# Splitting the second sum of a LayerNorm folding into pieces and spreading them over layer 0 of a two-way GRU

## The chip, the cores and the metric

The kernel runs on one core of a Trainium2 chip. The core has five engines with an instruction stream each: TensorE (PE in the profile; its weight loads are PEld), VectorE (DVE), ScalarE (ACT), GpSimd (POOL) and SyncE (SP), which issues nearly all DMAs. They run side by side and wait for one another through semaphores. The metric is the time of one execution on the device in microseconds (us), as the median of several runs; lower is better.

## What is computed

The input `x` has 8 sequences (b) of 512 tokens with 512 features. The block adds a fused two-way recurrent stack to it, and then a feed-forward part with ternary weights:

```python
def _mingru(x, Wz, bz, Wh, bh):
    z = sigmoid(x @ Wz.T + bz)
    h_tilde = tanh(x @ Wh.T + bh)
    a = clip(1.0 - z, 1e-8, 1.0 - 1e-8)
    return _linear_scan(a, z * h_tilde)        # h[t] = a[t] h[t-1] + z[t] h_tilde[t]

def _stack(x, ...):                            # 4 layers
    h = x
    for i in range(4):
        h_new = _mingru(h, Wz[i], bz[i], Wh[i], bh[i])
        if i > 0:
            h_new = h_new + h
        h = _layernorm(h_new, gamma, beta)
    return h

# block:
h_fwd = _stack(layernorm(x));  h_bwd = flip(_stack(flip(layernorm(x))))
x = x + concat(h_fwd, h_bwd) @ fusion_W.T + fusion_b
x = x + ffn(layernorm(x))                      # 512 -> 2048 -> gelu -> layernorm -> 512
```

All four weight and bias arguments of a layer are the same two arrays here, so one product serves the sigmoid and the tanh, and the two directions share it in layer 0.

## The kernel before

**Tiles and stages.** Features lie on the 128 partitions, in four chunks of 128; a tile is 128 features by 512 tokens in f32. Four stages follow one another: loads and the normalisation of `x` (to about 15 us), four recurrent layers for two sequences at a time with both directions, the fusion product, and the feed-forward part.

**One item of a layer** is a sequence, a direction and a layer: `layer(s, l)` with `s = (b, d)` (L541). It has four chunks, and each is one slot: four matmuls into an accumulator `u` in PSUM (L459), three activations on ScalarE that read it (`factors`, L473), and on VectorE a clamp, a product, a scan and an addition (L481 to L487, L552). Layer 0 has its own code (`first_layer`, L491), since both directions share the product: eight chunks for the first two sequences, `f0` and `f1`, each scaled by VectorE (L515) before the activations and scanned twice. The scaling of a chunk of `f1` comes two slots after its matmuls (`lag` 2), so its accumulator stays in use for that long.

**Normalisation.** The scanned tiles are transposed to token rows (`turned`, L307, into `pt`, two buffers), VectorE takes their statistics (L169), GpSimd the power (L176), ScalarE writes a normalised token tile (L187), which frees the `pt` buffer; then four token tiles are transposed back (`back`, L318, into `pf`, two buffers) and ScalarE writes them with `gamma` and `beta` applied (L329).

**The order of the work** is written out by hand (L114). `slot` (L437) emits a chunk's matmuls, then what `stages` holds as due (`factors`, `scans`, `resid`), then shares of the two queues `turns` and `backs`; `now` counts slots. `ready` (L251) lets no new token tile begin while ten are held (`held`, `TOK` = 10). The engines take their instructions in this order. Slots 0 to 7 are `f0 + f1` (L728); slots 8 to 11 are item (0, 0) of layer 1, 12 to 15 item (0, 1), and 16 begins item (1, 0).

**PSUM.** The pool `ps_u` (L229) has four buffers of one bank each. The accumulators of the layers, those of layer 0 and those of the folding all come from it.

**The folding.** The last layer's LayerNorm is not applied to the tokens. Instead its `gamma` goes into the fusion weights `fw`, its mean out of them, and its `beta` into the fusion bias. `both` (L119) is a table with `beta` and `gamma` of each feature repeated over 64 columns each, written by two VectorE copies after slot 7 (L730). `fold_sums(d)` (L667) multiplies it with the half of `fw` that belongs to direction d: four matmuls into `pfold`, then a ScalarE copy into a tile of the token pool. It is called after item (0, 0) and after item (0, 1) of layer 1 (L763). The products `pm` and `pb` (L682, L692) read both results in layer 2, from 145 us on.

**The first loads** on SP's queue are the weights and inputs of sequence 0, the GRU bias `gb`, four row tiles of sequence 1 (L148), its transposed input `xT` (L149), `gamma` and `beta` (L150), then the fusion bias and weights, the other layers' weights and the feed-forward's norm. Two VectorE statistics in the first slots read the first two of those row tiles. The program takes eight DMA completion semaphores in turn, so a load is issued once the load eight before it has landed.

Of the kernel before, what the change touches and what calls it, by code (L numbers as in the profile page):

```python
# [9 lines left out]
F32 = mybir.dt.float32  # L10
# [6 lines left out]
P = 128  # L17
# [7 lines left out]
def kernel(  # L25
# [26 lines left out]
    nc = tc.nc  # L52
    B, S, H = x.shape
    L = gru_wT.shape[0]
    F = fc_wT.shape[1]
    NC_ = H // P
# [13 lines left out]
    tokp = ctx.enter_context(tc.tile_pool(name="tok", bufs=TOK))  # L70
# [23 lines left out]
    def load_x(use, b, t):  # L94
        xs[use, b, t] = xsp.tile([P, H], F32, tag="xs", name=f"x{use}_{b}_{t}")
        nc.sync.dma_start(out=xs[use, b, t], in_=x[b, ts(t, P), :])
# [6 lines left out]
    def load_xT(b):  # L103
        xT[b] = hp.tile([P, NC_, S], F32, tag="h", name=f"xT_{b}")
        nc.sync.dma_start(out=xT[b], in_=xt[b].rearrange("(c p) s -> p c s", p=P))

    gb = const.tile([P, L, NC_], F32, name="gb")
    gam = const.tile([P, NC_], F32, name="gam")
    bet = const.tile([P, NC_], F32, name="bet")
# [9 lines left out]
    both = fusp.tile([P, NC_, 2, 64], F32, name="both")  # L119
    picks = []  # L120
    for i in range(2):
        s = fusp.tile([P, P], F32, name=f"fpick{i}")
# [17 lines left out]
    for first, second in (  # L140
# [3 lines left out]
        for q, (load, at) in ((nc.scalar, first), (nc.sync, second)):  # L144
            load(q, at)
    nc.sync.dma_start(out=gb, in_=gru_b)
    for t in range(NT):
        load_x("n", 1, t)  # L148
    load_xT(1)  # L149
    nc.sync.dma_start(out=gam, in_=gamma)  # L150
    nc.sync.dma_start(out=bet, in_=beta)
    fw = fusp.tile([P, 2 * NC_, H], F32, name="fw")
    nc.sync.dma_start(out=fb, in_=fus_b.broadcast_to([P, H]))
    nc.sync.dma_start(out=fw, in_=fus_wT.rearrange("(c p) h -> p c h", p=P))
# [72 lines left out]
    with rec:  # L227
        gp = rec.enter_context(tc.tile_pool(name="gate", bufs=3))
        ps_u = rec.enter_context(tc.tile_pool(name="ps_u", bufs=4, space=PSUM))  # L229
# [10 lines left out]
        held = [0]  # L240
# [232 lines left out]
        def factors(u, z, l, o, name):  # L473
            t = gp.tile([P, S], F32, tag="t", bufs=2, name=f"t_{name}")
            a = gp.tile([P, S], F32, tag="a", name=f"a_{name}")
            nc.scalar.activation(a, u, AF.Sigmoid, bias=ngb[:, l, o : o + 1], scale=-1.0)  # L476
            nc.scalar.activation(t, u, AF.Tanh, bias=gb[:, l, o : o + 1])  # L477
            nc.scalar.activation(z, u, AF.Sigmoid, bias=gb[:, l, o : o + 1])  # L478
            return a, t
# [11 lines left out]
        def first_layer(b, lag=0):  # L491


            zf, zb = [], []

            def chunk(o):
                def work():
                    while zlive[0] + 2 > ZT:
                        slot(None, 2)
                    zlive[0] += 2  # L500
                    name = f"{b}_0_{o}"
                    u = ps_u.tile([P, S], F32, tag="u", name=f"u_{name}")
                    for c in range(NC_):
                        nc.tensor.matmul(  # L504
                            u, lhsT=gw[0][:, c, ts(o, P)], rhs=xT[b][:, c, :],
                            start=(c == 0), stop=(c == NC_ - 1),
                        )
                        if (b, o, c) in midway:
                            midway.pop((b, o, c))()

                    wait = 1 if (b, o) == (0, 0) else 0

                    def scaled():
                        z = zp.tile([P, S], F32, tag="z", name=f"z_{name}")
                        nc.vector.tensor_tensor(z, u, scale[b], ALU.mult)  # L515
                        a, t = factors(z, z, 0, o, name)

                        def scans():
                            product(a, z, t)
                            f = zp.tile([P, S], F32, tag="z", name=f"zf_{name}")  # L520
                            scan(f, a, z, False)
                            zf.append(f)
                            if o == NC_ - 1:
                                state[b, 0] = xT.pop(b)
                                norm((b, 0), zf, f"{b}0_0", 2 if b == 1 else 1, 2 if b < 2 else 1)

                            def backward():
                                scan(z, a, z, True)
                                zb.append(z)
                                if o == NC_ - 1:  # L530
                                    norm((b, 1), zb, f"{b}1_0", 2 if b == 1 else 1, 2 if b < 2 else 1)
                            if b == 0:
                                stages.append((now[0] + 1, "resid", backward))
                            else:
                                backward()
                        stages.append((now[0] + 1 - wait, "scans", scans))
                    stages.append((now[0] + lag + wait, "factors", scaled))
                return work
            return [chunk(o) for o in range(NC_)]
# [124 lines left out]

        folded = {}

        def fold_sums(d):  # L667

            ps = ps_u.tile([P, H], F32, tag="u", name=f"pfold_{d}")
            for c in range(NC_):  # L670
                nc.tensor.matmul(
                    ps, lhsT=both[:, c, :, :].rearrange("p i r -> p (i r)"), rhs=fw[:, d * NC_ + c, :],
                    start=(c == 0), stop=(c == NC_ - 1),
                )
            folded[d] = tokp.tile([P, H], F32, tag="tok", name=f"fold_{d}")
            held[0] += 1
            nc.scalar.copy(folded[d], ps)

        def fold(d):

# [39 lines left out]
        end = take(xturns)  # L720
# [4 lines left out]
        take(xturns)  # L725
        midway[0, 1, 0] = lambda: take(xbacks)()
        f0, f1 = first_layer(0), first_layer(1, 2)
        for i, work in enumerate(f0 + f1):  # L728
            slot(work, 4 if i == NC_ + 1 else 2, i > NC_ + 1)
        for i, v in enumerate((bet, gam)):  # L730
            nc.vector.tensor_copy(both[:, :, i, :], v.unsqueeze(2).broadcast_to([P, NC_, 64]))
        for b in range(0, B, 2):
            last_pair = b + 2 == B
            if b == 0:
                for name, part in (("fc", fc_part), ("pw", proj_part)):
                    for i in range(NW):
                        absolute(part, i, name)
                    tots = []
                    extra.append([None, lambda n=name, tots=tots: tots.append(total(n))])
                    extra.append([None, lambda n=name, tots=tots: threshold(n, tots[0])])  # L740
                for name, part in (("fc", fc_part), ("pw", proj_part)):
                    for i in range(NW):
                        quantised(part, i, name)
            for l in range(1, L):
                if last_pair:
                    load_fc(l - 1)
                    if l == 1:
                        combined()
                        load_pw(0)
                for s in ((b, 0), (b, 1), (b + 1, 0), (b + 1, 1)):  # L750
                    if l == L - 1 and not last_pair and s[1] == 0:
                        norm_x(s[0] + 2, now[0])
                    if l == L - 1 and s[1] == 0:
                        load_pair("f", s[0])
                    if l == L - 2 and not last_pair and s[1] == 1:
                        load_pair("n", s[0] + 2)
                        load_xT(s[0] + 2)
                    if last_pair and s == (b, 1) and l == L - 2:
                        load_y(0)
                    if last_pair and s == (b, 0) and l == L - 1:  # L760
                        norm_y(0)
                    layer(s, l)
                    if b == 0 and l == 1 and s[0] == 0:  # L763
                        fold_sums(s[1])
                    if b == 0 and l == 2:
                        if s[0] == 0:
                            fold(s[1])
                        elif s[1] == 0:
                            fold_bias()
            if last_pair:  # L770
                load_fc(L - 1)


            firsts = [] if last_pair else first_layer(b + 2) + first_layer(b + 3)
            for i in range(2):
                for t, tile_ in enumerate(fusion(b + i)):
                    slot(tile_, 2, True)
                    for _ in range(2 if i == 0 and t % 2 == 0 else 1):
                        if firsts:
                            slot(firsts.pop(0))  # L780
                if last_pair and i == 0:
                    load_pw(1)
                    load_pw(2)
# [20 lines left out]
    for i in range(2):  # L804
        plain = tokp.tile([P, H], F32, tag="tok", name=f"plain{i}")[:, 0:P]
        nc.vector.memset(plain, 0.0)
        for j in range(2):
            r = 64 * i + 32 * j
            nc.vector.memset(plain[r : r + 1, :], 1.0)
        s = const.tile([P, P], F32R, name=f"pick{i}")  # L810
# [137 lines left out]
    for j in range(ends):  # L948
        b, k = divmod(j, NF)
# [81 lines left out]
```

## Time and profile before

| | |
|---|---|
| median of three runs | 1717.03 us (1716.73 to 1717.18) |
| the profiled execution: time, span of the core | 1717.09 us, 1715.1 us |
| PE busy | 1703.4 us, 99% of the span |
| DVE, ACT busy | 1452.0 us (85%), 1073.7 us (63%) |
| first sum of the folding: first matmul, ACT copy | 62.7 us, 66.4 us |
| second sum of the folding: first matmul, ACT copy | 87.4 us, 91.6 us |
| the two copies that write `both` | 47.3 us and 47.5 us, 0.28 us each |
| issue and landing of `gamma`, of `beta` | 11.7 to 17.3 us, 12.1 to 17.5 us |

The profile is of one execution. Its times are counted from the start of the span; the rest of an execution lies around the span. A line of the timeline or of the chain of work gives the start, the length, the engine, the line in the kernel, the operation and the tiles (written, then read), and in brackets how long the engine had been idle before and for whom it had waited. Buffer numbers are left out of tile names. A matmul of 128x512 in f32 shows as two instructions. Matmuls overlap, so their ends are modelled, and the busy share of PE says less than its waits.

### The profile page before, as it was taken

Reading aid. Unit: us, or ns where it says so; the run is one execution under the profiler, and the core shown is the slowest. Engines: PE = TensorE matmul, PEld = TensorE weight load, DVE = VectorE, ACT = ScalarE, POOL = GpSimd, SP = SyncE. Lnnn points to the kernel's source line nnn. Section 1 sums busy time; section 2 is a strip of 40 time slices with the busy share of each in tenths; the row PEclk is TensorE's granted clock in tenths of the full one; section 3 lists DMA queues with packets and bytes.
Section 4 is the critical chain, followed back from the end, with each engine's and each line's share of the span. In section 5 each row is a group of like instructions: output and inputs, shape, how many; then the busy total and the mean of one; then the engine's idle time right before and its main releaser. Section 6 shows DMA issues by size and latency. Waiting matters only on the chain.

```text
span 1715.1 us, 19769 instructions
## 1 busy us (share of the span) xinstructions
PE 1703.4 (99%) x6440; PEld 1042.3 (61%) x6440; DVE 1452.0 (85%) x2863; ACT 1073.7 (63%) x1856; POOL 214.0 (12%) x334
## 2 busy tenths in 40 slices
PE   9999999999999999999999999999999999999999
PEld 4455554555555445555545555554688888888887
DVE  7989989889998998999899899996568768768877
ACT  5898873468886246888624688860366566566654
POOL 2111111111111111111111111110000000000000
PEclk9999999999999999999999999999999999999999
DMA  7002221160000115000011201202201101100100
GB/s 270 19 25 81 99 86 43 56 202 1 1 13 19 56 56 202 1 1 18 14 55 68 105 9 41 74 1 96 76 1 49 50 0 50 49 16 35 50 19 32
DMA packets 46599, 91.75 MB, mean 53 GB/s; under 512 B 5280, under 2 KB 5536, under 8 KB 45472
## 3 DMA queue, kind: packets, MB, share of 16 engines
q1 hardware_dynamic: 45488, 88.78, 15.1%
q10 hardware_dynamic: 1008, 1.70, 0.3%
q8 instruction: 51, 0.84, 0.2%
q14 instruction: 52, 0.43, 0.1%
HBM read 65.30 MB, written 25.17 MB: 53 GB/s over the span
## 4 chain that ended last, share of the span: by engine, by line
PE 87%; DVE 10%; ACT 1%; issue 1%; DMA 1%; POOL 0%; DVEq 0%; ACTq 0%
PE u L459 32%; PE po L870 14%; PE ph L843 14%; PE pu L586 12%; PE pt L314 6%; PE u L504 5%; PE pf L323 4%; DVE z L487 3%; DVE st L169 1%; DVE z L483 1%; PE py L212 1%; DVE zf L487 1%; DVE z L552 1%; DVE a L482 1%; DVE mv L171 0%
## 5 line engine op out<-in xcount | busy, mean ns | idle before, releaser
L459 PE MATMUL u<-h,gw 128*128 128x512 f32 x768 | 345.5, 592 | 0.0
L459 PE MATMUL u<-xT,gw 128*128 128x512 f32 x768 | 345.4, 593 | 0.0
L487 DVE TENSOR_TENSOR_SCAN z<-a,z 128x512 f32<-128x512 f32 x224 | 274.1, 1224 | 7.6
L459 PEld LDWEIGHTS u<-h,gw 128*128 128x128 f32 x768 | 138.7, 190 | 139.2 <-issue 138.9
L459 PEld LDWEIGHTS u<-xT,gw 128*128 128x128 f32 x768 | 138.7, 190 | 139.2 <-issue 138.2
L476 ACT ACTIVATE a<-u,ngb 128x512 f32<-128x512 f32 x192 | 131.6, 685 | 142.4 <-PE u L459 141.8
L169 DVE BATCH_NORM_STATS2 st<-pt 128x6 f32<-128x512 f32 x256 | 177.2, 692 | 40.8 <-PE pt L314 40.3
L176 POOL TENSOR_TENSOR rs<-ve,mhalf 128x1 f32<-128x1 f32 x192 | 122.7, 639 | 703.7 <-DVE nmu L180 665.4
L870 PE MATMUL po<-pwq,ghi 128*128 128x512 f32 x512 | 202.7, 396 | 0.0
L843 PE MATMUL ph<-yhi,fcq 128*128 128x512 f32 x512 | 199.7, 390 | 0.0
L870 PE MATMUL po<-pwq,glo 128*128 128x512 f32 x512 | 199.6, 390 | 0.0
L843 PE MATMUL ph<-ylo,fcq 128*128 128x512 f32 x512 | 199.4, 389 | 0.0
L847 ACT ACTIVATE g<-ph 128x512 f32<-128x512 f32 x128 | 76.4, 597 | 186.4 <-PE ph L843 186.4
L483 DVE TENSOR_TENSOR z<-z,t 128x512 f32<-128x512 f32 x224 | 153.4, 685 | 9.4 <-ACT z L478 9.4
L187 ACT ACTIVATE tok<-pt,nmr,rs 128x512 f32<-128x512 f32 x192 | 149.2, 777 | 6.4
L858 DVE TENSOR_TENSOR acc<-acc,g 128x512 f32<-128x512 f32 x112 | 77.3, 690 | 84.7 <-ACT g L847 83.8
L478 ACT ACTIVATE z<-u,gb 128x512 f32<-128x512 f32 x192 | 132.2, 689 | 0.0
L477 ACT ACTIVATE t<-u,gb 128x512 f32<-128x512 f32 x192 | 130.7, 681 | 0.0
L314 PEld LDWEIGHTS pt<-ident,z 128*128 128x128 f32 x640 | 78.6, 141 | 80.2 <-issue 47.5
L504 PE MATMUL u<-xT,gw 128*128 128x512 f32 x256 | 115.0, 593 | 1.0 <-DVE gw L716 0.8
L586 PE MATMUL pu<-fw,xT 128*128 128x512 f32 x256 | 115.2, 593 | 0.0
L586 PE MATMUL pu<-fw,h 128*128 128x512 f32 x256 | 115.1, 592 | 0.0
(150 smaller groups left out, 2559.8 us busy)
## 6 DMA issues: line engine op xcount, KB each, us to landing
xf<-in_x_dram SPq DMA_DIRECT2D x32, 256.0 KB, 5.8
x<-xf SPq DMA_DIRECT2D x32, 256.0 KB, 2.0
xy<-x SPq DMA_DIRECT2D x32, 256.0 KB, 4.1
xn<-in_x_dram SPq DMA_DIRECT2D x31, 256.0 KB, 4.5
out_dram<-xy SPq DMA_DIRECT2D x31, 256.0 KB, 2.0
xT<-in_xt_dram SPq DMA_DIRECT2D x7, 1024.0 KB, 7.5
fca<-in_fc_wT_dram SPq DMA_DIRECT2D x16, 256.0 KB, 3.0
pwa<-in_proj_wT_dram SPq DMA_DIRECT2D x16, 256.0 KB, 2.7
```

The lines of the kernel that those rows point to most:

```text
L169: nc.vector.bn_stats(st, src)
L187: nc.scalar.activation(dst, src, AF.Identity, bias=nmr, scale=rs)
L314: nc.tensor.transpose(pt[:, ts(c, P)], zs[c][:, ts(t, P)], ident)
L459: nc.tensor.matmul(u, lhsT=gw[l][:, c, ts(o, P)], rhs=h[:, c, :], start=(c == 0), stop=(c == NC_ - 1),)
L476: nc.scalar.activation(a, u, AF.Sigmoid, bias=ngb[:, l, o : o + 1], scale=-1.0)
L478: nc.scalar.activation(z, u, AF.Sigmoid, bias=gb[:, l, o : o + 1])
L483: nc.vector.tensor_tensor(z, z, t, ALU.mult)
L487: nc.vector.tensor_tensor_scan(dst[:, d], a[:, d], z[:, d], 0.0, ALU.mult, ALU.add)
L504: nc.tensor.matmul(u, lhsT=gw[0][:, c, ts(o, P)], rhs=xT[b][:, c, :], start=(c == 0), stop=(c == NC_ - 1),)
L586: nc.tensor.matmul(pu, lhsT=hs[d][:, c, ts(t, P)], rhs=fw[:, d * NC_ + c, :], start=(c == 0), stop=(c == NC_ - 1),)
L843: nc.tensor.matmul(ph, lhsT=w, rhs=ys[b][c][i], start=(c == 0 and i == 0), stop=(c == NC_ - 1 and i == 1),)
L870: nc.tensor.matmul(po[b][t], lhsT=part[:, ts(t, P)], rhs=pwq[k // NP_][:, k % NP_, :], start=(k == 0 and i == 0), stop=(k == NF - 1 and i ...
```

## The change

The second half of the folding, `fold_sums(1)`, no longer comes as one block after item (0, 1) of layer 1. Its four matmuls go in three places: c = 0 and 1 directly behind the matmuls of layer 0's chunk (1, 2) in slot 6, c = 2 behind those of chunk (1, 3) in slot 7, and c = 3 after the whole first sum, behind item (0, 0) of layer 1. They add into one accumulator, which is taken in slot 6 and read by its ScalarE copy after c = 3. The result is held among the token tiles from then on, one item sooner than before.

For this the table `both` has to be ready in slot 6. Its two copies move from the end of slot 7 to the scaling of the first chunk of all, and the loads of `gamma` and `beta` move ahead of sequence 1's rows and its `xT` on SP's queue.

```diff
     nc.sync.dma_start(out=gb, in_=gru_b)
+    nc.sync.dma_start(out=gam, in_=gamma)
+    nc.sync.dma_start(out=bet, in_=beta)
     for t in range(NT):
         load_x("n", 1, t)
     load_xT(1)
-    nc.sync.dma_start(out=gam, in_=gamma)
-    nc.sync.dma_start(out=bet, in_=beta)
...
                         a, t = factors(z, z, 0, o, name)
+                        if wait:
+                            for i, v in enumerate((bet, gam)):
+                                nc.vector.tensor_copy(both[:, :, i, :], v.unsqueeze(2).broadcast_to([P, NC_, 64]))
...
-        def fold_sums(d):
-
-            ps = ps_u.tile([P, H], F32, tag="u", name=f"pfold_{d}")
-            for c in range(NC_):
+        fold_ps = {}
+
+        def fold_sums(d, cs=range(NC_)):
+
+            for c in cs:
+                if c == 0:
+                    fold_ps[d] = ps_u.tile([P, H], F32, tag="u", name=f"pfold_{d}")
                 nc.tensor.matmul(
-                    ps, lhsT=both[:, c, :, :].rearrange("p i r -> p (i r)"), rhs=fw[:, d * NC_ + c, :],
+                    fold_ps[d], lhsT=both[:, c, :, :].rearrange("p i r -> p (i r)"), rhs=fw[:, d * NC_ + c, :],
                     start=(c == 0), stop=(c == NC_ - 1),
                 )
-            folded[d] = tokp.tile([P, H], F32, tag="tok", name=f"fold_{d}")
-            held[0] += 1
-            nc.scalar.copy(folded[d], ps)
+            if c == NC_ - 1:
+                folded[d] = tokp.tile([P, H], F32, tag="tok", name=f"fold_{d}")
+                held[0] += 1
+                nc.scalar.copy(folded[d], fold_ps[d])
...
         f0, f1 = first_layer(0), first_layer(1, 2)
+        def with_sums(work, d, cs):
+
+            def go():
+                end = work()
+                fold_sums(d, cs)
+                return end
+            return go
+
+        f1[2] = with_sums(f1[2], 1, (0, 1))
+        f1[3] = with_sums(f1[3], 1, (2,))
         for i, work in enumerate(f0 + f1):
             slot(work, 4 if i == NC_ + 1 else 2, i > NC_ + 1)
-        for i, v in enumerate((bet, gam)):
-            nc.vector.tensor_copy(both[:, :, i, :], v.unsqueeze(2).broadcast_to([P, NC_, 64]))
...
-                    if b == 0 and l == 1 and s[0] == 0:
-                        fold_sums(s[1])
+                    if b == 0 and l == 1 and s == (0, 0):
+                        fold_sums(0)
+                        fold_sums(1, (3,))
```

## The prediction

> **What bounds the kernel now.** I read the summary first. TensorE (PE) is busy 1703.4 us of a span of 1715.1, so at most 11.7 us can be had from filling its gaps, and the change removes no PE work; it moves four matmuls (c = 0 to 3 of the folding's second sum).
>
> ```profile
> span 1715.1 us, 19769 instructions
> PE 1703.4 (99%) x6440; PEld 1042.3 (61%) x6440; DVE 1452.0 (85%) x2863; ACT 1073.7 (63%) x1856; POOL 214.0 (12%) x334
> ```
>
> Next the waits of PE between 30 and 100 us, where the edits lie (columns: total us, times, longest):
>
> ```profile
> PE pt L314 <- ACT tok L187: 1.8, 4, 0.6
> PE pt L314 <- DVE z L487: 1.7, 1, 1.7
> PE pf L323 <- ACT tok L187: 0.4, 1, 0.4
> PE pf L323 <- ACT h L329: 0.2, 1, 0.2
> ```
>
> That is 4.1 us, over a third of all idle PE time. Each wait is for something that VectorE (DVE) or ScalarE (ACT) delivers late. The chain of work, followed from 8 to 100 us and then once more from its end for 80 to 102 us, says why (start, us, what; two answers, so two fences):
>
> ```profile
> 21.43 0.15 DVE ve_x L383
> 21.58 0.33 DVE a L482
> ...
> 47.38 0.40 DVE both L731 x2
> ```
>
> ```profile
> 86.05 0.66 PE pt L314 x4
> 86.71 0.87 PE pf L323 x8
> 87.58 3.44 PE pfold L671 x8
> 91.02 3.43 PE u L459 x8
> ```
>
> From 21.43 us the chain is DVE without a break into the seventies, the two table copies (0.40 us) included. DVE has no idle time worth naming until 91.8 us. From 86.05 on it is PE, and the second sum's 3.44 us stand on it. The timeline shows the change of hands: DVE waits 3.13 us for PE behind that sum, and after 100 us all PE waits to the end of the run are 1.4 us. So: **a stretch set by DVE and ACT to about 87 us, one set by PE after it.** Moving 3.44 us of PE work from the second into the first pays as far as the first has room.
>
> ```profile
> 38.25 0.76 PE L314 MATMUL pt<-ident,z 128*128 128x128 f32 x5 [1.73 <-DVE z L487]
> 50.93 3.60 PE L459 MATMUL u<-xT,gw 128*128 128x512 f32 x8
> 51.31 0.70 ACT L478 ACTIVATE z<-u,gb 128x512 f32<-128x512 f32 x1
> 70.88 0.69 DVE L169 BATCH_NORM_STATS2 st<-pt 128x6 f32<-128x512 f32 x1
> 94.92 0.70 DVE L169 BATCH_NORM_STATS2 st<-pt 128x6 f32<-128x512 f32 x1 [3.13 <-PE pt L314]
> ```
>
> [...] before, no accumulator `u` waits for a bank, but the change takes one of four away for five slots. [...] gamma and beta go in pieces of 16 B. [...] 385 GB/s falls to between 242 and 333 from 16 to 18 us, when both land.
>
> **Part by part.** Each 128x512 f32 matmul is two instructions 0.43 us apart: 0.86 us.
>
> *Removed after item (0,1):* 8 x 0.43 = 3.44 us of PE on the path, and one ACT copy (0.57 us) beside it.
>
> *Pieces 0 and 1, behind the matmuls of layer 0's chunk (1, 2):* +1.72 us from about 36.0. Next on PE are four transposes of z, the fourth waiting for a scan until 38.25, a gap of 1.73. Three of them, 0.11 each, end by 38.1 instead of 36.4: cost 0. Without that gap they would cost 1.72.
>
> *Piece 2, behind chunk (1, 3):* +0.86 from 43.8 to 44.6. The transposes behind it wait until 44.03 for a buffer anyway. Their first result comes about 0.6 us after they start, at 45.3, and DVE wants it at 45.0: DVE loses 0.3. PE itself regains step at 50.3, where it waits for a token.
>
> *Table copies:* -0.40 us of DVE at 47.4. They go behind the first scaling (ends 15.6), where DVE waits 1.27 us for PE until 16.87: 2 x 0.285 fit. They now wait for gamma and beta, which must have landed by about 16.2 (see the DMAs), and the next chunk's scaling stands behind them. With piece 2 DVE is 0.1 us ahead, but at 52.06 it meets ACT, whose z for the first item of layer 1 ends at 51.31 + 0.70 = 52.01, out of an ACT sequence unbroken since 38.57. Nothing of the 0.1 survives.
>
> *The bank.* The pool hands out the bank that was released first in program order; the banks of the compiled program before follow that rule through the first fifty accumulators. With one held by the open sum, item 0's second chunk of layer 1 gets the bank of its first chunk, which ACT has read at 52.01, instead of one free long before. PE would start it at 50.93 and starts about 52.1: +1.1 us. Behind it on PE are two rows of transposes that waited on ACT for 0.25 and 0.17 us; after them 0.6 us of delay is left. Bounds: 0 (another free bank is taken) to 4.4 (the chunk that DVE reads last, until 55.33).
>
> *Piece 3, behind the first sum:* +0.86, so item (0,1) starts 0.6 + 0.86 = 1.46 us late. DVE wants its first transposes at 70.88; they start 69.59 + 1.46 = 71.05 and are ready about 0.6 later, 71.65: DVE slips 0.75 and carries that to 87 us. PE's own lag beyond it goes into the token waits at 75.2 and 80.4.
>
> *The handover.* PE at 87.58 + 0.75 goes straight to the next item: 3.44 - 0.75 = 2.7 us ahead. But the 3.44 us were also a breather. DVE, done at 91.79 + 0.75, is 2.4 ahead. ACT has two tokens and a weight row to finish until 92.5 where it started at 94.49: 2.0 ahead. The second transposes of each following slot have about 0.3 us of slack to their token (99.66 against 99.9). So PE keeps 2.0 + 0.3 = 2.3; from 110 us slots have half the transposes and ACT and DVE catch up. The copy moved to the first sum falls in 2.85 us of idle ACT; it costs 0.57 if ACT were full there.
>
> *DMAs.* On SP the two small loads go ahead of four row loads and `xT`(1). Before, the rows are issued at 8.12, 8.8, 9.1 and 10.3 and land 4.0 to 4.4 later, the first two at 12.2 and 12.9. DVE reads them at 12.68 and 13.68. SP's pace is set by earlier loads landing, so rows take later turns (first two about 9.1 and 10.3), but with 512 KB less ahead of them. The dip above is (66 + 52 + 90 + 143) x 0.5 us = 175 KB missed, 0.46 us. So they land near 12.6 and 13.3: just in time. Gamma and beta, behind `gb` (lands 11.95), land near 12.5. Cost 0, bounds 0 and 0.8; a loss would be whole, as DVE's first scaling waits behind these rows and ACT's sequence to 21.4 behind it. The load of `xT`(1) then lands near 17.3, wanted after 20; later loads keep their turns.
>
> *Planner.* The second folded tile is held four slots sooner. In slot 15 tokens reach 1 + 4 + 4 = 9 before; with one more the last check sees 9, under 10, so nothing is put off: cost 0 (a slot of about 5 us for one turn if it did).
>
> **Sum.** -3.44 + 0.75 + 0.4 = -2.3 us. Profiled: 1717.09 us, 2.0 around its span; span 1715.1 - 2.3 = 1712.8. It stands at the median of the runs, 1717.03: **1714.7**.
>
> **Rivals.**
> B. No bank wait: the sum leaves nearly whole. Then DVE slips only 0.2 at 70.88 and the result is -3.44 + 0.2 + 0.25 = -3.0, to -4.0 if DVE's 0.4 survives too: in the middle 1713.5. For it: a bank freed at 48.4 is there. Against: it is second in line.
> C. The sum was cover anyway: ACT, unbroken from 94.5 to 112, becomes the bound and gives the rest back; 0 to -1, 1716.5. For it: 0.3 us of slack. Against: PE has no listed wait from 94 to 200 us.
> D. Slower: the same second chunk gets the bank that DVE reads last and waits to 55.33, 4.4 us; the delay at 70.88 is the wait less 0.35, and the gain is gone at a wait of 3.4. At 4.4: +1.0, 1718.0. For it: nothing in the waits of before excludes it, since no bank was short there. Against: its release comes later in the program than the other two.
>
> **How the numbers follow.** A 0.52, B 0.26, C 0.10, D 0.12. A alone spans 1713.5 to 1716.2 (bank wait 0.5 to 2, rows late up to 0.8). A change of 0.2%, 3.43 us, is about what a measurement of this kernel can tell from none: below 1713.6 lie 0.15 of B and 0.09 of A; above 1720.5 lies 0.08 of D, if the next chunks wait as well. The range runs from the far end of B, 1713.0, over C to the near side of D, 1717.5; about 0.05 of B below and 0.12 of D and of late rows above are left out.
>
> **What would show it.** Right: the gap of 1.73 near 38 us gone, `pfold` pieces near 36, 44 and 66; the PE start at 50.9 moved to 52.1 with a wait on ACT's z; statistics near 70.9 late by 0.7; the 3.13 us wait at 94.9 gone. Wrong: `u` waiting elsewhere, rows read after 12.7, tokens holding PE from 94 to 112 us by more than half a microsecond.

## The result, and the profile after

The changed kernel takes 1714.84 us (median; 1714.64 to 1715.16), the kernel before, run beside it, 1717.01 us (1716.73 to 1717.92). The ratio is 0.9987, with a 95% interval of 0.9981 to 0.9993: 2.17 us less, or 0.13%, and 0.1 us from the 1714.7 of the prediction. Between the two profiled executions the span falls from 1715.1 to 1712.8 us.

First the summary of the profile after:

```profile
span 1712.8 us, 19767 instructions
PE 1702.2 (99%) x6440; PEld 1041.8 (61%) x6440; DVE 1452.1 (85%) x2863; ACT 1074.3 (63%) x1856; POOL 214.5 (13%) x334
```

PE, DVE, ACT and POOL have as many instructions as before. What changed is waiting. The waits of PE after, between 30 and 100 us (total us, times, longest):

```profile
PE u L459 <- ACT z L478: 1.0, 1, 1.0
PE pt L314 <- ACT tok L187: 0.9, 2, 0.6
PE pf L323 <- ACT tok L187: 0.4, 1, 0.4
```

They add up to 2.3 us where they were 4.1. The 1.7 us for DVE's scan are gone, the four token waits are two, and a wait has come that was not there: an accumulator `u` waits 1.0 us for a bank. The list accounts for 1.8 of the 2.3 us by which the span fell; where the rest lies it does not show (the busy time of PE, whose ends are modelled, is 1.2 us lower for the same instructions). Beyond 100 us the waits are 1.4 us in both kernels, line by line the same.

The chain of work after, from 60 to 100 us (start, us, what):

```profile
63.47 4.29 PE pfold L677 x10
67.76 3.43 PE u L459 x8
71.19 0.45 PE pt L314 x4
71.67 0.71 DVE st L169
...
96.76 0.79 ACT tok L187
97.59 0.66 PE pt L314 x4
98.25 0.88 PE pf L323 x8
```

Before, the chain was on DVE in the sixties, PE came onto it at 86.05 and the second sum (3.44 us) stood on it. Now PE is on it from 52.03, where the wait for the bank ends, through the first sum and piece 3 at 63.47 (five matmuls, 4.29 us). It hands over to DVE at 71.67; the chain stays there until 94.76, passes to ACT, and comes back to PE at 97.59, after a token that ACT writes. So PE takes over for good some eleven microseconds later than before, and no sum stands behind that point.

The timeline after, in the order of the prediction's steps (start, us, engine, line, operation; in brackets the idle time before it):

```profile
12.57 0.69 DVE L169 BATCH_NORM_STATS2 st_x<-xn 128x6 f32<-128x512 f32 x1
...
35.93 1.88 PE L677 MATMUL pfold<-fw,both 128*128 128x512 f32 x4
37.65 1.32 PE L314 MATMUL pt<-ident,z 128*128 128x128 f32 x8
...
45.22 0.70 DVE L169 BATCH_NORM_STATS2 st<-pt 128x6 f32<-128x512 f32 x1 [0.16 <-PE pt L314]
...
51.28 0.70 ACT L478 ACTIVATE z<-u,gb 128x512 f32<-128x512 f32 x1
52.03 3.70 PE L459 MATMUL u<-xT,gw 128*128 128x512 f32 x8 [0.97 <-ACT z L478]
...
71.67 0.70 DVE L169 BATCH_NORM_STATS2 st<-pt 128x6 f32<-128x512 f32 x1 [0.76 <-PE pt L314]
...
88.23 3.60 PE L459 MATMUL u<-xT,gw 128*128 128x512 f32 x8
...
92.38 0.68 ACT L476 ACTIVATE a<-u,ngb 128x512 f32<-128x512 f32 x1
...
98.96 3.60 PE L459 MATMUL u<-xT,gw 128*128 128x512 f32 x8
```

Two lines of the kernel before stand beside the last matmuls:

```profile
90.85 3.60 PE L459 MATMUL u<-xT,gw 128*128 128x512 f32 x8
...
101.22 3.60 PE L459 MATMUL u<-xT,gw 128*128 128x512 f32 x8
```

The pieces fill the gap that was at 38 us, and the eight transposes then run through. `u` starts at 52.03 instead of 50.93, because ACT's read of the item's first chunk ends only then. DVE waits 0.76 us at 71.67. The matmuls that began at 90.85 before begin at 88.23, 2.62 us earlier; those of 101.22 begin at 98.96, 2.26 us earlier, and that lead holds: the chunk of 110.27 begins at 108.02. Such leads are good to about 0.2 us. DVE's first scaling starts at 14.91 us in the profile of the kernel before, at 14.81 in that of the changed kernel, and at 14.69, 14.72, 14.78 and 14.89 in those of again, e1, e7 and e2_table. e4, where nothing is changed ahead of the second sum, is as far off: its transposes just ahead of the sum start at 85.86 where those of the kernel before start at 86.05.

### The profile page after: what moved, and what is told of

It reads as the page before. It is cut to its first block, busy times and chain, and to the rows that moved or that the text cites. A ratio compares the mean times of both kernels' runs of the same rounds, so it can differ in the third digit from the quotient of the medians.

```text
span 1712.8 us, 19767 instructions
## 1 busy us (share of the span) xinstructions
PE 1702.2 (99%) x6440; PEld 1041.8 (61%) x6440; DVE 1452.1 (85%) x2863; ACT 1074.3 (63%) x1856; POOL 214.5 (13%) x334
## 4 chain that ended last, share of the span: by engine, by line
PE 88%; DVE 9%; ACT 1%; DMA 1%; issue 1%; POOL 0%; DVEq 0%; ACTq 0%
PE u L459 33%; PE po L886 14%; PE ph L859 14%; PE pu L589 12%; PE pt L314 5%; PE u L504 5%; PE pf L323 4%; DVE z L487 2%; DVE st L169 2%; DVE z L483 1%; PE py L212 1%; DVE z L555 1%; DVE a L482 1%; DVE zf L487 1%; DVE mv L171 0%
```

## The experiments

The experiments take the terms of the prediction's sum one by one, against its rivals B (the bank costs nothing), C (the sum was cover) and D (a longer wait for the bank), and against one that it did not name: that something else in the change made the gain, such as the moved table or loads. Each kernel was timed beside the kernel before on the same chip. The medians of the kernel before in the four series are 1717.34 us (again, e1, e7, e3), 1717.27 (e2_table, e4, e5, e6), 1717.06 (e2_repeat, e8, e9) and 1717.11 (e10). The first two are the higher ones, and their series have the larger share of the longer executions that the last section tells of (16 of 54 and 16 of 49, against 8 of 38 and 2 of 17), so versions of different series can be set against each other only to about 0.3 us.

**The changed kernel once more (again).**

> The changed kernel once more, as the yardstick for the three beside it: about 2.2 us under the kernel before, PE waiting about 1.0 us for ACT's z before the second chunk of layer 1's first item, DVE's statistics near 70.9 late by about 0.75 us.

1714.98 us (1714.84 to 1715.46), ratio 0.9986 [0.998, 0.9993], span 1712.9. The gain repeats: 2.4 us. For e1, e7 and e3, timed in the same series, this run is the yardstick.

**The bank (e1_bank).** Only the order of releases in the program changes. The scaling of chunk (1, 2), which frees its accumulator, is recorded before the slot's matmuls and not behind them. The order of the instructions on each engine stays as it was.

```diff
         def slot(work=None, cap=1, long=False):
 
+            due("early")
             end = work() if work is not None else None
...
-                    def scaled():
+                    made = []
+
+                    def scaling():
+                        if made:
+                            return made[0]
                         z = zp.tile([P, S], F32, tag="z", name=f"z_{name}")
                         nc.vector.tensor_tensor(z, u, scale[b], ALU.mult)
+                        made.append(z)
+                        return z
+
+                    def scaled():
+                        z = scaling()
...
+                    if (b, o) == (1, 2):
+                        stages.append((now[0] + lag, "early", scaling))
```

> Only the order of two releases is changed: the scaling of layer 0's chunk (1, 2) is written ahead of the first item's first chunk in the program; each engine's own order stays. The second chunk then gets the bank that VectorE has read by 48.4 us. Theory (the bank wait is late work that DVE pays for at 70.9): no PE wait at 51 us, DVE late by 0.2 instead of 0.75 at 70.9, PE at the next item 0.5 us earlier than in the changed kernel; 2.8 us under the kernel before. Rival (the wait is swallowed by the token waits behind it): same as the changed kernel, 2.2 under.

1714.38 us (1714.22 to 1714.69), ratio 0.9982 [0.9975, 0.9989], span 1712.3: 0.6 us under the changed kernel. The timeline of e1:

```profile
50.82 3.60 PE L460 MATMUL u<-xT,gw 128*128 128x512 f32 x8
...
71.00 0.70 DVE L169 BATCH_NORM_STATS2 st<-pt 128x6 f32<-128x512 f32 x1
```

The wait of 0.97 us is gone and DVE is 0.67 us earlier at 71. In the changed kernel too the scaling of chunk (1, 2) ended at 48.2 us (47.51 + 0.68), and yet PE waited to 52.03 for another bank. So the bank was handed out by its place in the program and not by the time it came free, and 0.6 us of the result is its price. The near end of rival B, -3.0 us, describes this kernel and not the changed one.

**The bank and piece 3 (e7_both).** e1, and piece 3 goes behind the matmuls of the second chunk of item (0, 1).

```diff
+                work = gates(h, l, o, f"{s[0]}{s[1]}_{l}_{o}", scans)
+                slot(with_sums(work, 1, (3,)) if (s, l, o) == ((0, 1), 1, 1) else work)
...
                     if b == 0 and l == 1 and s == (0, 0):
                         fold_sums(0)
-                        fold_sums(1, (3,))
```

> As the order of releases changed, and the fourth piece goes behind the matmuls of chunk 1 of item (0, 1) instead of behind the first sum. Theory: DVE isn't late at 70.9 at all, and the 0.86 us of PE vanish in the token wait near 80.4; PE at the next item 3.4 us earlier than before, of which ACT takes some 0.4 back by 100 us; 3.0 under the kernel before (1.7 if the piece only moves the lateness to the next statistics). Rival (ACT sets 94 to 112 us and has no more to give): 2.2 to 2.4 under.

1714.13 us (1714.03 to 1714.52), ratio 0.998 [0.9972, 0.9988], span 1712.1. The timeline of e7, and behind it two lines of the kernel before:

```profile
70.82 0.69 DVE L169 BATCH_NORM_STATS2 st<-pt 128x6 f32<-128x512 f32 x1
...
73.86 1.02 PE L690 MATMUL pfold<-fw,both 128*128 128x512 f32 x2
...
75.62 3.60 PE L460 MATMUL u<-h,gw 128*128 128x512 f32 x8
...
80.34 0.66 PE L314 MATMUL pt<-ident,z 128*128 128x128 f32 x4 [0.60 <-ACT tok L187]
```

```profile
75.18 0.66 PE L314 MATMUL pt<-ident,zf 128*128 128x128 f32 x4 [0.59 <-ACT tok L187]
...
75.67 3.60 PE L459 MATMUL u<-h,gw 128*128 128x512 f32 x8
```

DVE has its statistics at 70.82, as in the kernel before (70.88). Piece 3 at 73.86 is paid from the token wait near 75: before, PE waits 0.59 us there, in e7 not at all, and the matmuls behind start at 75.62 where they started at 75.67. The wait near 80.4, which the expectation named, is untouched (0.60 us, 0.59 before). With this the slip at 70.88 is accounted for within the spread of the profiles: 0.67 us (71.67 to 71.00) from the bank and 0.18 (71.00 to 70.82) from the place of piece 3.

**The whole sum behind the first (e3_behind_first).** Table and loads as in the changed kernel, but the four pieces together after item (0, 0).

```diff
-        f1[2] = with_sums(f1[2], 1, (0, 1))
-        f1[3] = with_sums(f1[3], 1, (2,))
...
-                        fold_sums(1, (3,))
+                        fold_sums(1)
```

> Table and loads early, all four matmuls of the second sum behind the first sum, no open sum across slots. Theory (only room in front of a late DVE pays): DVE wants its first statistics of item (0, 1) at 70.9, they come at 73.6, it slips 2.7 us and PE keeps 0.3 to 0.7; 0.4 us under the kernel before. Rival (anything moved ahead of 87 us is free, because DVE sets that stretch): 2.3 to 3.4 under.

1717.47 us (1716.84 to 1717.69), ratio 0.9999 [0.9991, 1.0007]: no gain where 0.4 us was expected. The profiled execution has a span of 1714.8, 0.3 under the kernel before. Its timeline says where the sum went:

```profile
73.49 0.70 DVE L169 BATCH_NORM_STATS2 st<-pt 128x6 f32<-128x512 f32 x1 [2.72 <-PE pt L314]
```

A block of 3.44 us moved to 66 us stops DVE for 2.72 us there. So the earlier place does not pay by itself; what is moved has to fit the waits that are there. The sum of this run is 3.44 - 2.6 (DVE's 73.49 against 70.88) - 0.4 at the handover = 0.4, of which 0.3 is in the profile. Eight of the thirteen executions of e3 show a lower mean clock (0.999), which the last section comes to; whether that alone takes the rest is not shown.

**The sum left out (e4_left_out).** The kernel before without the second sum: its four matmuls and its copy are left out, and the result of the first stands in for it.

```diff
         def fold_sums(d):
 
+            if d == 1:
+                folded[1] = folded[0]
+                return
...
-            held[0] -= 2
+            held[0] -= 1
```

> The kernel before without the second sum: its four matmuls and its copy are left out, and the first sum's result stands in for it. Theory: 3.44 us leave the path at 87 us, ACT is only 2.7 us earlier since it has two tokens and a weight row to finish, PE keeps 0.35 us more than ACT; 3.0 us faster than before, and no placement of the pieces can give more. Rivals: the whole 3.44 (the sum covered nothing), or under 1 (it was cover for ACT and DVE).

1714.04 us (1713.71 to 1715.33), ratio 0.9982 [0.9975, 0.9988], span 1711.9. The timeline of e4:

```profile
87.23 3.60 PE L459 MATMUL u<-xT,gw 128*128 128x512 f32 x8
...
97.95 3.60 PE L459 MATMUL u<-xT,gw 128*128 128x512 f32 x8
```

PE is 3.62 us ahead of the kernel before at 87.23 and 3.27 at 97.95, which is what stays; 0.2 us of both was there before the edit acts (85.86 instead of 86.05 for the transposes). So the sum really lay on the path, about nine tenths of it; C, by which at most 1 us was to be had, falls. It also bounds what moving the sum alone can give: 3.2 us or a little less. The changed kernel gets 2.3 of that in its profile, e7 3.0.

**The table and its loads alone (e2_table, e2_repeat).** The two copies and the loads of `gamma` and `beta` as in the changed kernel, the second sum as before. Run twice.

```diff
-        f1[2] = with_sums(f1[2], 1, (0, 1))
-        f1[3] = with_sums(f1[3], 1, (2,))
...
-                    if b == 0 and l == 1 and s == (0, 0):
-                        fold_sums(0)
-                        fold_sums(1, (3,))
+                    if b == 0 and l == 1 and s[0] == 0:
+                        fold_sums(s[1])
```

> Only the table's copies and the loads of gamma and beta are moved; both sums stay whole and where they were. Theory: the 0.40 us that leave DVE at 47.4 end at ACT's z near 52.0, and the rows land just in time; 0 us against the kernel before, plus or minus 0.3. Rivals: DVE's 0.4 survive, 0.4 us faster; or the rows land late, 0.3 to 0.8 slower.

> The same kernel as the one with only the table and the loads moved, since that execution's profile had a PE delay of about 0.7 us near 44 us that no wait explains. Theory: 0 us against the kernel before, plus or minus 0.3; without that delay DVE's statistics near 70.9 are where they were, within 0.2 us, and the 0.40 us are lost at ACT's z near 52.0.

1717.34 us (1716.95 to 1717.93), ratio 1.0001 [0.9993, 1.0009], and 1717.18 (1717.07 to 1717.95), ratio 1.0 [0.9991, 1.0008]. Moving the table gains nothing by itself. The repeat was made to be rid of a delay of PE that the first profile shows near 44 us, and has it too: the two profiled executions have spans of 1715.8 and 1715.7, 0.7 and 0.6 above the kernel before. The stretches of e2_table say where it comes from (from:to, length, then busy us and instructions of PE, PEld, DVE, ACT, POOL, the granted clock of PE, DMA share, GB/s):

```profile
40.00:42.00 2.00, 2.00 (x7) 1.21 (x6) 1.86 (x7) 1.97 (x4) 1.06 (x2) 0.54 0.00 0
42.00:44.00 2.00, 2.00 (x4) 0.87 (x3) 1.93 (x4) 1.97 (x5) 0.00 (x0) 0.61 0.00 0
```

The granted clock of PE fell to 0.54 and 0.61 from 40 to 44 us; in e2_repeat it was 0.87, 0.50 and 0.78 in the three stretches from 38 us. Nothing in the edit asks for that, which led to e10.

**The gap filled with work that nobody reads (e10_filled).** e2_table, and behind the matmuls of chunk (1, 2) two matmuls into an accumulator that is read by nothing: the same 1.72 us of PE as pieces 0 and 1, in the same place, and the sum itself not moved. It only adds work.

```diff
+        def filled(work):
+
+            def go():
+                end = work()
+                fill = ps_u.tile([P, H], F32, tag="u", name="fill")
+                for c in range(2):
+                    nc.tensor.matmul(
+                        fill, lhsT=both[:, c, :, :].rearrange("p i r -> p (i r)"), rhs=fw[:, NC_ + c, :],
+                        start=(c == 0), stop=(c == 1),
+                    )
+                return end
+            return go
+
+        f1[2] = filled(f1[2])
```

> Only the table and the loads moved, and two matmuls whose result nobody reads put behind chunk (1, 2), into the gap of 1.7 us; both sums whole and where they were. Theory (PE's gap near 38 us is what lets the granted clock fall for the next 3 us in some executions, about half of those of the kernel before and of the one without the filler): all executions lie in the lower group, 1716.9 to 1717.3, none above 1717.5, and the clock is 1.00 from 38 to 46 us. Rival (the clock falls for another reason): two groups as before, the upper about 0.6 to 1.0 us higher.

1717.01 us (1716.92 to 1717.42), ratio 0.9999 [0.9991, 1.0008], span 1715.0. Twelve of its thirteen times lie at or below 1717.12; one is 1717.42, above what was expected, at a mean clock of 1.00. Of the 26 of e2_table and e2_repeat eleven lie above 1717.5. The stretch of e10, with the columns as above, and a line of its timeline:

```profile
40.00:42.00 2.00, 2.00 (x9) 1.04 (x8) 1.86 (x7) 1.97 (x4) 0.90 (x2) 1.00 0.00 0
```

```profile
51.91 0.69 DVE L483 TENSOR_TENSOR z<-z,t 128x512 f32<-128x512 f32 x1 [0.31 <-ACT z L478]
```

Three things follow. Two pieces in the gap cost nothing: 1.72 us more of PE and no change of time. With the gap filled the profile shows a clock of 1.00, and one execution of 13 a mean of 0.999 instead of nine of 26; but these three runs were made on three chips, so what the gap has to do with it rests on the wider count of the last section. And of the 0.40 us that DVE saves by the moved copies 0.31 turn up as a wait for ACT's `z` at 51.9, as the prediction's step on the table has it.

**Pieces 0 and 1 one slot earlier (e6_slot5).** Behind chunk (1, 1), where PE has no gap.

```diff
-        f1[2] = with_sums(f1[2], 1, (0, 1))
+        f1[1] = with_sums(f1[1], 1, (0, 1))
```

> Pieces 0 and 1 one slot earlier, behind chunk (1, 1), where PE has no gap; all else as in the changed kernel. Theory: DVE's statistics at 32 us come 1.1 us late, DVE and ACT carry that to 87 us, and part of the gap near 38 us stays open; 1.2 us under the kernel before. Rival (the gap does not matter, PE catches up at 38 us): 2.2 under.

1716.13 us (1715.93 to 1716.45), ratio 0.9993 [0.9985, 1.0002], span 1713.9: half of the gain is gone. The timeline of e6:

```profile
32.98 0.70 DVE L169 BATCH_NORM_STATS2 st<-pt 128x6 f32<-128x512 f32 x1 [1.06 <-PE pt L314]
...
39.24 0.76 PE L314 MATMUL pt<-ident,z 128*128 128x128 f32 x5 [1.23 <-DVE z L487]
```

DVE waits 1.06 us for the transposes that now stand behind the pieces, and PE's gap stays, 1.23 us of it, one us later. The wait for the bank is that of the changed kernel (1.0 us for ACT's `z`), so it is not what costs more here. The same two matmuls cost 0 in slot 6 and 1.1 in slot 5.

**Two more small loads ahead of the rows (e5_loads).** The changed kernel, with `gamma` and `beta` loaded a second time into tiles that are not read.

```diff
     nc.sync.dma_start(out=gam, in_=gamma)
     nc.sync.dma_start(out=bet, in_=beta)
+    for i, v in enumerate((gamma, beta)):
+        nc.sync.dma_start(out=const.tile([P, NC_], F32, name=f"again{i}"), in_=v)
     for t in range(NT):
         load_x("n", 1, t)
```

> The changed kernel with gamma and beta loaded a second time into tiles that nobody reads, also ahead of sequence 1's rows. Theory: the rows are only just in time; two more turns and 0.4 us more of small pieces bring the first row from 12.5 to about 13.0 us, DVE's first scaling comes 0.4 us later and the loss is whole: 1.8 us under the kernel before. Rival (there is room at the start): as the changed kernel, 2.2 under.

1715.95 us (1715.38 to 1716.44), ratio 0.9992 [0.9984, 1.0], span 1713.9: some 1.0 us more than the changed kernel (1.1 in the span), and not 0.4. SP's queue in e5, and DVE beside it:

```profile
9.11 0.43 SPq L150 DMA_DIRECT2D again<-in_gamma_dram  x1
10.08 0.33 SPq L150 DMA_DIRECT2D again<-in_beta_dram  x1
10.46 2.43 SPq L96 DMA_DIRECT2D xn<-in_x_dram  x4
```

```profile
13.41 0.69 DVE L171 BATCH_NORM_STATS2 st_x<-xn 128x6 f32<-128x512 f32 x1 [0.72 <-DMA xn<-in_x_dram]
...
14.90 0.69 DVE L171 BATCH_NORM_STATS2 st_x<-xn 128x6 f32<-128x512 f32 x1 [0.39 <-DMA xn<-in_x_dram]
```

The rows' issue went from 9.13 to 10.46: 0.43 + 0.33 us for issuing the two loads, and 0.54 us between them in which the queue stood. The first row lands 2.9 us after its issue. In the changed kernel the first row lands at about 12.5 and is read at 12.57, so there was no room, and the loss is whole: DVE stands 0.72 and 0.39 us and has its first scaling at 15.91 instead of 14.81. The two loads of the change themselves cost nothing only because they end just there.

**A pass of ACT out of the handover (e9_row, e8_row).** At the end of item (0, 1) of layer 1 ACT also makes a pass over one tile of the feed-forward's weights (L620, 0.6 us at 91.77). It goes to layer 2's item (1, 0), in e9 with the changed kernel and in e8 with e7.

```diff
-                if s[0] < 2 and (l == L - 1 or o % 2) and len(extra) > 2 * NW or s == (B - 1, 1) and l == L - 1:
-                    pieces(1)
+                if (s, l, o) == ((0, 1), 1, 3):
+                    pass
+                elif s[0] < 2 and (l == L - 1 or o % 2) and len(extra) > 2 * NW or s == (B - 1, 1) and l == L - 1:
+                    pieces(2 if (s, l, o) == ((1, 0), 2, 3) else 1)
```

> The changed kernel with only that weight-row pass moved. Theory: PE keeps the 2.6 us that it has at the next item's start instead of 2.25; 0.3 faster than the changed kernel, 2.6 under the kernel before. Rival: as the changed kernel, 2.2 to 2.4 under.

> The kernel with the releases reordered and the fourth piece behind item (0, 1)'s chunk 1, and besides one of ACT's weight-row passes (0.8 us) moved from the end of item (0, 1) to layer 2. Theory (ACT's late start takes 0.3 to 0.4 us back after 91 us): the token wait near 97 us goes, PE is 3.4 to 3.5 us earlier for good; 0.2 to 0.3 faster than without that move, 3.4 under the kernel before. Rival (DVE takes it back): no change, 3.2 under.

e9: 1714.56 us (1714.43 to 1714.89), ratio 0.9985 [0.9978, 0.9991], span 1712.6. e8: 1713.73 (1713.61 to 1714.14), ratio 0.9979 [0.997, 0.9988], span 1711.7. Two lines of the timeline of e9, then one of e8:

```profile
96.80 1.04 PE L314 MATMUL pt<-ident,z 128*128 128x128 f32 x8
...
98.55 3.60 PE L459 MATMUL u<-xT,gw 128*128 128x512 f32 x8
```

```profile
101.13 1.04 PE L314 MATMUL pt<-ident,z 128*128 128x128 f32 x8
```

In e9 eight transposes run through at 96.80, where the changed kernel stops behind four until ACT's token ends at 97.55, and PE keeps 2.67 us (101.22 before) where the changed kernel keeps 2.26; in e8 it keeps 3.52 (104.65 before). So ACT was the taker of the prediction's last 0.4 us: with its 0.6 us pass elsewhere those come back. In the time it is less sure: the span of e9 is 0.2 us under the changed kernel's, its median 0.3 to 0.4, on another chip. e8 is the best of all versions: 3.3 us under the kernel before and some 1.1 under the changed one.

## Why the prediction was right

The forecast, 1714.7, is 0.1 us from the result, and the sum behind it, -3.44 + 0.75 + 0.4, holds term by term, each for the reason that it gave. Some side remarks do not hold. By its steps:

- **The sum was on the path.** Right: without it the time falls by 3.2 us (e4), and C falls with that.
- **Pieces 0 and 1 in the gap, cost 0.** Right: shown by e10 (0) against e6 (1.1 us in a slot without the gap).
- **Piece 2, DVE loses 0.3.** Right in kind, a little too large: DVE waits 0.16 us and starts at 45.22, 0.2 later than before. It has no effect: DVE takes up ACT's z at 52.01, as soon as ACT has written it.
- **The table's 0.40 us lost at ACT's z.** Right: e2 gains nothing, and e10 shows 0.31 of it as a wait.
- **The bank.** Right in place and cause: PE starts at 52.03 (52.1 said), after a wait of 0.97, and e1 prices it at 0.6. It was a single wait, and not one for want of a bank: e1, with one held just as long, does not wait (its `u` starts at 50.82). B is refuted by the same pair of runs. Its far end, -4.0, was also more than its terms give: -3.0 with DVE's 0.4 added is -3.4.
- **Piece 3 and the slip at 70.88.** Right: 71.67 where 71.65 was said. e1 and e7 split it into 0.67 us for the bank and 0.18 for piece 3. PE's own lag went into the token wait near 75 alone; the one near 80.4, which the prediction also names, stays at 0.59 us.
- **The handover.** Right: PE is 2.62 ahead (2.7 said), ACT begins at 92.38 (92.5 said), PE keeps 2.26 (2.3 said), and the pass over the weights is what ACT lacked the time for (e9). Rival C named the right engine with the wrong size: 0.4 of the 2.7 us given back, and not 1.7 or more.
- **The DMAs.** Right in the outcome, off in a size and in a reason. The second row lands at 12.9, not 13.3, and the `xT` of sequence 1 at 18.2, not 17.3, which nothing waits for. The prediction argued with bytes ahead in the queues and laid the dip in the DMA rate at 16 to 18 us on the small pieces of `gamma` and `beta`. That is not shown: in the changed kernel both have landed by 12.3 us, and between 17.5 and 19 us the rate still falls to between 127 and 213 GB/s. The turns do follow the landings: in the kernel before the issue of `gamma` waits 0.6 us for a part of `xT`, in the changed kernel that of `beta` 0.4 us for a row tile. In e5 it is the turn on SP's queue that moved the rows, which land 2.9 us or more after their issue. The expectation of e5 was 0.6 us short for that reason.
- **The planner, cost 0.** Right: up to 180 us PE, apart from the sums, takes its groups of matmuls in the order of before.
- **D, a wait until 55.33.** Did not come: the bank was that of the first chunk, which ACT had read at 51.98.

What the prediction did not have is the granted clock, told below. It hardly shows in the medians compared here (two of the 22 times of the kernel before lie above 1717.5).

## What to carry to other kernels

Where the profile shows that the bounding engine changes in the course of a kernel, look for waits of the second engine in the first one's stretch, and for pieces of its work that fit them: here the same 3.44 us gave 2.3 us in pieces and at most 0.3 as a block. Here the accumulator held open over several slots took a bank from the rotation, and a wait of 0.97 us fell on the chunk that was handed the next bank by program order; recording a release earlier cost nothing and gave 0.6 us back. Once a stretch is shortened, look for what the next engine does there that can be done elsewhere: here one 0.6 us pass of ACT, worth 0.2 to 0.4.

## What was not expected of the hardware

Kernels that leave PE's gap near 38 us open (the kernel before, with 1.73 us, e2, e3, e4) have executions that are longer by about 0.5 to 1.5 us than the rest. Of the kernel before, 16 of 54, 16 of 49, 8 of 38 and 2 of 17 times lie above 1717.7 in the four series, and the others at or below 1717.6. All these longer ones show a mean granted clock of 0.999; so do 14 of the others. Counted by that clock, the kernels with the gap have it in 76 of 218 executions, on four chips. Those with the gap filled or shortened (the changed kernel, again, e1, e5 to e10) have it in 4 of 144 on the same chips and in the first series, with times among those of the rest. The closest pair is e3 and again, on one chip and alike except for the place of the second sum's matmuls: 8 of 13 against 1 of 21. The clock fell in two profiles, those of e2: to 0.54 and 0.61 in the stretches from 40 to 44 us of e2_table, and to 0.87, 0.50 and 0.78 in those from 38 to 44 of e2_repeat. In e2_table the gap stands shortly before:

```profile
38.28 0.76 PE L314 MATMUL pt<-ident,z 128*128 128x128 f32 x5 [1.78 <-DVE z L487]
...
40.53 5.11 PE L504 MATMUL u<-xT,gw 128*128 128x512 f32 x8
```

Eight such instructions take 3.60 us in the kernel before (at 40.33). Their weight loads come 0.43 us apart there, and 0.85 apart from 41.39 to 43.09 in e2_table, which is half the rate. As an estimate, the 1.51 us by which the eight take longer make about 3 us of it. Ahead of the fall stand 1.78 us without a matmul and, shortly after, 0.39 us of waiting (PE is busy for 1.8 of the 4 us from 36 to 40). They do not bring it every time: in the profiled executions of the kernel before, e3 and e4 the gap is 1.73, 1.8 and 1.7 us, PE is busy for 1.8 to 1.9 of these 4 us, and the clock stays at 1.00. With 1.23 us left of the gap (e6) all 13 executions have a mean of 1.00. That the gap has a part in the fall is read from the counts alone. Whether its length decides, and whether the short waits around it count, is not shown, nor what makes the four exceptions; nor was the fall seen in a profile of the kernel before itself. As an estimate from the first of the four series, it costs that kernel 0.3 us on average (16 of 54 times, 1.0 us each), a part of the gain that no wait in its profile shows. It may also be why e3, with 8 of 13 such executions, lies above what was expected of it.
